# The first layer's seven products of pair 1 issued ahead of the last products with values

## The chip, the cores and the metric

The kernel runs on one core of a Trainium2 chip. The metric is the device time of one execution in microseconds (us), lower being better. The core has four computing engines that work side by side, each strictly through its own list of instructions: TensorE (PE in the profile; PEld is its loading of weights), VectorE (DVE), ScalarE (ACT) and GpSimd (POOL). SyncE (SP) issues most transfers (DMAs), also in a fixed order. An instruction that waits holds up everything behind it in its own list.

## The reference

All numbers are float32. A batch of 32 sequences of 112 rows (x, width 256) attends to its own context of 375 rows, with 16 heads of 64; then a mixture of 8 experts, two for each row, is added. Cut to what matters:

```
def xattn(ctx, latents):                  # latents: x after a normalisation
    q = lat @ Wq
    k, v = split(concat([ctx_normed, lat]) @ Wkv)
    attn = softmax(q k^T * scale)
    return (attn @ v) @ Wout

x = x + tanh(g_xattn) * xattn(ctx, layernorm(x))

xf = layernorm(x)                         # 3584 rows
top2 of softmax(xf @ gate_w), renormalised
h = gelu(xf @ w1[e] + b1[e])              # 256 -> 1024
y = h @ w2[e] + b2[e]                     # 1024 -> 256
x = x + tanh(g_ffn) * (sum of the two experts' y, weighted)
```

## The kernel before

The kernel has two stages that overlap at their seam.

**Attention** is a loop over 128 units `n` (32 sequences of 4 units). A unit computes scores, a softmax in the tile `ex`, and a transposition of it that goes through memory: `send_blocks(n)` writes `ex` to the memory tile `turned` in four DMAs (L526), `take_blocks(n)` reads it back as `exT[n]` (L533). `attend(j)` then makes the products with values for two units, 2j and 2j+1, into the PSUM tile `ps_o` (L546), and ScalarE copies the result to `outT` (L563). `project(i)` multiplies a slab of 128 rows of `outT` by Wout (L583), and `residual(i)` adds it to x on VectorE (L593), takes the row statistics (L241, L242), sends the slab to `out` on SyncE (L596), and leaves a root for GpSimd (L603, L605). When a slab is done its rows are routed: gate scores, the two best experts, places in the lists of the experts (among them the small matmuls L693 and L694, which need counts from GpSimd, L686), and a scatter of the rows to the memory tile `xg`.

**Experts** work on blocks of rows from `xg`, in pairs of blocks, 256 rows. Pair 0 is computed plainly (`hidden_plain`, L1047; `second_plain`, L1062), inside and just behind the last units of attention. Pairs 1 to 20 use a scheme with seven half-sized products in place of eight, in both layers:

- `fetch_rows(t)` reads a pair's rows into `xs` (L934); `turn_rows(t)` transposes them on TensorE (L1022) and copies them to `xsT` (L1026), on VectorE for pairs 1 and 2 and on ScalarE after that;
- `rows_sums(t)` makes the four sums `xt` on GpSimd (L1038);
- `fetch_first(t)` issues the seven weight tiles of the first layer (`w`, `w_s`, L987), behind a read of the biases (L948), all on SyncE; a tile has one buffer, so the fetch for pair t+1 waits for the products of pair t;
- `hidden_pair(t)` makes seven products (L1111, four matmuls each, all in PSUM tiles of one tag with four buffers), one copy on ScalarE (L1121), seven adds on VectorE (L1122 to L1130) and eight Gelus on ScalarE (L1118);
- `hidden_sums`, `second_pair`, `out_pair` and `fetch_second` do the same for the second layer; for pair 0 `combine(0)` ends the work (L1095, L1096, and the scatter L1072).

After the pairs come single blocks. The order of the work on every engine is written out by hand: the program order of the calls is the order on each engine. Between the attention loop and the loop over pairs stands the stretch that is changed. `pieces_of(6)` in that loop runs six more small parts of the routing of the last two slabs. `now()` empties the list of postponed GpSimd operations. The pair loop begins, for t = 1, with

```
hidden_pair(t)
fetch_first(t + 1)
turn_rows(t + 1, nc.scalar.copy if t > 1 else None)
if t + 1 < PAIRS:
    rows_sums(t + 1)
pieces_of(6)
```

In the last two turns of the attention loop the transfers on SyncE are, in order: block 126 of `exT`, the first-layer weights of pair 1, the four writes of block 127, its read into `exT`, and the second-layer weights of pair 1 with the rows of pairs 2 and 3.

Of the kernel before, what the change touches and what calls it, by code (L numbers as in the profile page):

```python
# [23 lines left out]
def kernel(  # L24
# [152 lines left out]
    if True:  # L177
# [360 lines left out]
        def attend(j):  # L538

            g, i = divmod(j, NG)  # L540
            ps = ps_m.tile([P, 2, 2 * S], F32, tag="m", name=f"ps_o_{j}")
            for r in range(2):
                for x in range(2):
                    for c, (_, m) in enumerate(keys):
                        for y in range(2):
                            nc.tensor.matmul(  # L546
                                ps[y * DH : (y + 1) * DH, r, x * S : (x + 1) * S].rearrange(
                                    "p (a i) -> p a i", a=QB
                                ),
                                lhsT=vv[j][:m, c, x, r, y * DH : (y + 1) * DH],  # L550
                                rhs=exT[2 * j + x][:m, :, r, c, y, :Q],
                                start=(c == 0),
                                stop=(c == NCK - 1),
                            )

            t, end = 2 * g * S, 2 * (g + 1) * S
            while t < end:
                slab, at = divmod(t, P)
                n = min(P - at, end - t)
                if slab not in outT:  # L560
                    outT[slab] = soft.tile([P, NP, P], F32, tag="outT", name=f"outT_{slab}", bufs=3)
                o = t - 2 * g * S
                nc.scalar.copy(outT[slab][:, i::NG, at : at + n], ps[:, :, o : o + n])  # L563
                t += n
# [9 lines left out]
        def project(i):  # L574

            g, j = group[i]
            if j == 0:
                xr[g] = rows.tile([P, groups[g], 2, C], F32, tag="xr", name=f"xr_{g}")
                nc.gpsimd.memset(xr[g][:, :, :, D + 2 :], 0.0)
            ps_p[i] = ps_m.tile([P, D], F32, tag="m", name=f"ps_p_{i}")  # L580
            heads = outT.pop(i)
            for c in range(NP):
                nc.tensor.matmul(  # L583
                    ps_p[i],
                    lhsT=heads[:, c, :],
                    rhs=wo_sb[:, c, :],
                    start=(c == 0),
                    stop=(c == NP - 1),
                )
# [376 lines left out]
        def fetch_first(t):  # L966

            e, new = found["e", t] = expert_of(t)
            fetch_biases(t, e, found["weights"], 2, (0,))
            if t < PAIRS:  # L970
                s1_, s2_, s3_, s4_ = (
                    (f"s{n + 1}", ws1[bass.ds(e, 1), place].rearrange("o p f -> p (o f)"))
                    for n, place in enumerate((3, 0, 1, 2))
                )
                a11, a12, a22 = (
                    (n, half_of_w1(e, k, h)) for n, k, h in (("11", 0, 0), ("12", 1, 0), ("22", 1, 1))
                )
                order_ = (a11, s2_, s3_, s1_, a22, a12, s4_)
            else:
                if t == PAIRS:  # L980
                    new_weights("21", [P, 512], "s3")
                order_ = [
                    (n, half_of_w1(e, k, h))
                    for n, k, h in (("11", 0, 0), ("12", 1, 0), ("21", 0, 1), ("22", 1, 1))
                ]
            for n, src in order_:
                nc.sync.dma_start(wt[n], src, **new)  # L987
# [29 lines left out]
        def turn_rows(t, copy=None):  # L1017
            n = 2 if t < PAIRS else 1
            ps = ps_m.tile([P, KD, n, P], F32, tag="m", name=f"ps_x_{t}")
            for k in range(KD):  # L1020
                for b in range(n):
                    nc.tensor.transpose(ps[:, k, b, :], xs[t][:, b, k * P : (k + 1) * P], ident)  # L1022
            xsT[t] = found["tiles" if t > 0 else "early"].tile(
                [P, KD, 2, P], F32, tag="xsT", name=f"xsT_{t}"
            )
            (copy or nc.vector.tensor_copy)(xsT[t][:, :, :n, :], ps)  # L1026

        def rows_sums(t):

            x = xsT[t]  # L1030
            v = xt[t] = found["tiles"].tile([P, 4, P], F32, tag="xt", name=f"xt_{t}")
            for o, l, r in (
                (v[:, 0], x[:, 0, 1], x[:, 0, 0]),
                (v[:, 1], x[:, 1, 1], v[:, 0]),
                (v[:, 2], x[:, 1, 1], x[:, 0, 1]),
                (v[:, 3], x[:, 1, 0], v[:, 1]),
            ):
                nc.gpsimd.tensor_tensor(o, l, r, ALU.subtract)  # L1038
# [19 lines left out]
        def second_plain(b):  # L1058
            banks.append(banks.pop(0))
            ps = psy[0, b] = banks[-1][:, 0, :D]  # L1060
            for f in range(NF):
                nc.tensor.matmul(  # L1062
                    ps,
                    lhsT=hid[0][:, f, b, :],
                    rhs=found["w2"][:, f, :],
                    start=(f == 0),
                    stop=(f == NF - 1),
                )
# [31 lines left out]
        def hidden_pair(t):  # L1100


            h = hid[t] = found["tiles"].tile([P, NF, 2, P], F32, tag="h", name=f"h_{t}")
            x, v = xsT[t], xt[t]
            H = NF // 2
            h11, h12, h21, h22 = (h[:, i : i + H, b, :] for i in (0, H) for b in range(2))

            def product(n, w, r):
                ps = ps_m.tile([P, H, P], F32, tag="m", name=f"ps_h_{t}_{n}")
                for c in range(H):  # L1110
                    nc.tensor.matmul(  # L1111
                        ps[:, c, :], lhsT=wt[w][:, c * P : (c + 1) * P], rhs=r, start=True, stop=True
                    )
                return ps

            def gelu(lo):
                for f in range(lo, lo + H):
                    nc.scalar.activation(h[:, f], h[:, f], AF.Gelu, bias=bias[t][0][:, f : f + 1])  # L1118

            add = nc.vector.tensor_tensor  # L1120
            nc.scalar.copy(h11, product(1, "11", x[:, 0, 0]))  # L1121
            add(h12, product(6, "s2", v[:, 1]), h11, ALU.add)  # L1122
            add(h21, product(7, "s3", v[:, 2]), h12, ALU.add)
            ps = product(5, "s1", v[:, 0])
            add(h22, ps, h21, ALU.add)
            add(h12, ps, h12, ALU.add)  # L1126
            add(h21, product(4, "22", v[:, 3]), h21, ALU.add)
            gelu(H)
            add(h11, product(2, "12", x[:, 1, 0]), h11, ALU.add)
            add(h12, product(3, "s4", x[:, 1, 1]), h12, ALU.add)  # L1130
            gelu(0)
# [224 lines left out]
        def do(parts):  # L1356
            for part in parts:
                part()
# [251 lines left out]
        def pieces_of(n):  # L1610
            for _ in range(min(n, len(todo))):
                do(todo.pop(0))

        now()
        for b in range(2):
            second_plain(b)
        attend(LAST // 2 - 1)
        for u in range(2):
            project(i + u)
        rows_sums(1)  # L1620
        for u in range(2):
            residual(i + u)
            now()
        for t in range(1, PAIRS):
            hidden_pair(t)
            fetch_first(t + 1)
            turn_rows(t + 1, nc.scalar.copy if t > 1 else None)
            if t + 1 < PAIRS:
                rows_sums(t + 1)
            pieces_of(6)  # L1630
            hidden_sums(t)
            if t > 1:
                second_pair(t - 1)
                out_pair(t - 1)
                fetch_second(t)
            else:
                combine(0)
                do(found.pop("sums"))
            if t + AHEAD == EARLY:
                pieces_of(len(todo))  # L1640
                do(outgoing)
                del outgoing[:]
            if t + AHEAD == EARLY + 1:
                for e in range(E):
                    r = number("behind", 0, e, PADS)
                    nc.sync.dma_start(xg[bass.ds(r, P), :], pad)
            fetch_rows(t + AHEAD)
            if outgoing:
                outgoing.pop(0)()
# [65 lines left out]
```

## Time and profile before

| what | value |
|---|---|
| time of three runs | 2052.3, 2056.42, 2056.62 us (median 2056.42) |
| the profiled execution | 2051.52 us, of which its span is 2049.8 us |
| mean granted clock of TensorE | 0.987 of full speed |
| TensorE busy | 1960.6 us, 96% of the span |
| VectorE, ScalarE, GpSimd busy | 66%, 56%, 48% |
| memory traffic | 211 GB/s on average over the span |
| TensorE waiting for the last transposed block in the products with values | 6.63 us, once |

Durations that follow are those of the one profiled execution. A timeline row gives the start in us from the span's start, the duration, engine, line of the kernel, operation, the tile written and the tiles read (numbers of buffers left out), the type and the count of instructions merged into the row; brackets hold the idle time of the engine before it and who ended that. A matmul in float32 is recorded as two instructions. A row by stretches gives how long each engine was busy within the stretch, then the clock granted to TensorE (1.00 is full speed), the share of the DMA engines in use and what they moved.

### The profile page before, as it was taken

What the parts mean: (1) busy time and instruction counts of PE and PEld (TensorE: products, weight loads), DVE (VectorE), ACT (ScalarE), POOL (GpSimd) and SP (SyncE); (2) the same over time, 40 slices, a digit from 0 to 9 for tenths busy, and PEclk for the clock granted to TensorE, in tenths of its full rate; (3) what the DMA queues carried; (4) which work ended last, traced back from release to release, by engine and by line L of the source; (5) the groups of instructions that cost most, each with busy time, mean ns of one, the idle gap of its engine ahead of it and who ended that gap; (6) DMA issues with size and microseconds to landing.
All of it is one profiled execution on the core that took longest, in us unless ns stands there. A gap on an engine that the chain in (4) does not pass through costs nothing. (4 is left out here: it accounts for less than half of the span.)

```text
span 2049.8 us, 41104 instructions
## 1 busy us (share of the span) xinstructions
PE 1960.6 (96%) x14352; PEld 1501.5 (73%) x14352; DVE 1348.0 (66%) x2417; ACT 1155.5 (56%) x2718; POOL 992.3 (48%) x1467
## 2 busy tenths in 40 slices
PE   8999999999999999999999999999988799799998
PEld 4676767676667676766777676667766799799887
DVE  6777776868776767677777777786764476455211
ACT  5666666566666656666666666666644234344333
POOL 5534333435355645655456646542332377757322
PEclk9999999999999999999999999999998899999999
DMA  7766665666687878788778878875666476599773
GB/s 215 204 214 198 181 201 170 190 180 202 192 247 216 270 214 249 231 254 234 231 224 250 242 227 232 260 201 165 200 191 201 127 222 176 148 326 294 203 222 53
DMA packets 261057, 433.40 MB, mean 211 GB/s; under 512 B 30729, under 2 KB 149073, under 8 KB 244465
## 3 DMA queue, kind: packets, MB, share of 16 engines
q1 hardware_dynamic: 248384, 414.37, 67.7%
q0 software_dynamic: 11328, 15.33, 3.9%
q8 instruction: 115, 1.88, 0.4%
q10 hardware_dynamic: 1136, 1.05, 0.2%
q14 instruction: 94, 0.76, 0.1%
HBM read 301.37 MB, written 172.28 MB: 231 GB/s over the span
## 5 line engine op out<-in xcount | busy, mean ns | idle before, releaser
L501 ACT ACTIVATE ex<-bank,nmx 128x512 f32<-128x512 f32 x512 | 348.3, 689 | 264.3 <-DVE nmx L492 264.3
L515 ACT ACTIVATE ex<-ex,rc 128x512 f32<-128x512 f32 x512 | 342.5, 720 | 202.9 <-DVE rc L512 201.3
L492 DVE TENSOR_REDUCE nmx<-bank 128x2 f32<-128x974 f32 x256 | 286.1, 1158 | 122.7 <-PE bank L482 122.7
L520 DVE STREAM_TRANSPOSE ex<-ex 128x1024 f32<-128x1024 f32 x256 | 315.0, 1230 | 28.4 <-ACT ex L515 28.4
L422 POOL TENSOR_TENSOR kT<-tmpk,kT 128x487 f32<-128x487 f32 x63 | 76.9, 1220 | 376.9 <-ACT kT L440 376.9
L412 PEld LDWEIGHTS ps_v<-wkv_s,tT 128*128 128x128 f32 x1536 | 190.1, 192 | 79.4 <-DVE kT L446 37.4
L482 PE MATMUL bank<-kT,qTs 64*128 64x487 f32 x1024 | 243.7, 594 | 0.0
L546 PE MATMUL ps_o<-exT,vv 128*64 128x112 f32 (+1 forms) x4096 | 213.7, 262 | 7.9 <-DMA exT<-turned 6.6
L412 PE MATMUL ps_v<-wkv_s,tT 128*128 128x128 f32 x1536 | 199.9, 278 | 13.2 <-DVE kT L446 11.7
L546 PEld LDWEIGHTS ps_o<-exT,vv 128*64 128x64 f32 (+1 forms) x4096 | 199.5, 137 | 16.3 <-DMA exT<-turned 6.8
L446 DVE TENSOR_TENSOR vv<-ps_v,vv 128x512 f32<-128x512 f32 x192 | 131.8, 687 | 108.1 <-PE ps_v L412 87.1
L406 PE MATMUL ps_k<-tT,wkv_s 128*128 128x487 f32 x378 | 181.0, 583 | 13.8 <-DVE vv L446 13.1
L412 PEld LDWEIGHTS ps_v<-wkv,kvT 128*128 128x128 f32 x1024 | 129.7, 192 | 72.9 <-issue 66.2
L422 POOL TENSOR_TENSOR vv<-tmpv,vv 128x512 f32<-128x512 f32 x64 | 81.4, 1271 | 188.3 <-ACT vv L440 188.0
L1072 POOL DMA_INDIRECT out_dram<-y,xs x60 | 93.4, 1557 | 162.0 <-DVE y L1096 92.2
L482 PEld LDWEIGHTS bank<-kT,qTs 64*128 64x128 f32 x1024 | 88.1, 186 | 103.3 <-issue 92.4
L446 DVE TENSOR_TENSOR kT<-ps_k,kT 128x487 f32<-128x487 f32 x189 | 123.3, 657 | 31.3 <-PE ps_k L406 26.1
L1300 POOL TENSOR_TENSOR piece<-piece 128x128 f32<-128x128 f32 x256 | 116.9, 457 | 55.1 <-DMA piece<-in_L_ffn_w_dram 39.3
L412 PE MATMUL ps_v<-wkv,kvT 128*128 128x128 f32 x1024 | 141.8, 282 | 0.0
L406 PE MATMUL ps_k<-kvT,wkv 128*128 128x487 f32 x252 | 130.2, 598 | 0.0
L333 PE MATMUL ps_q<-kvT,wq_sb 128*128 128x224 f32 x512 | 120.0, 356 | 1.4 <-ACT kvT L321 0.7
L1118 ACT ACTIVATE h<-h,b 128x256 f32<-128x256 f32 x160 | 66.2, 495 | 97.1 <-DVE h L1126 67.6
(296 smaller groups left out, 3689.2 us busy)
## 6 DMA issues: line engine op xcount, KB each, us to landing
turned<-ex SPq DMA_DIRECT2D x512, 256.0 KB
exT<-turned SPq DMA_DIRECT2D x128, 1024.0 KB
w<-in_L_ffn_w_dram SPq DMA_DIRECT2D x132, 256.0 KB
w_s<-ws SPq DMA_DIRECT2D x80, 256.0 KB
w_t<-ws SPq DMA_DIRECT2D x80, 256.0 KB
w_b2x<-in_L_ffn_w_dram SPq DMA_DIRECT2D x38, 512.0 KB
ws<-piece SPq DMA_DIRECT2D x64, 256.0 KB
cin<-in_ctx_dram SPq DMA_DIRECT2D x32, 336.0 KB
```

Source lines behind the costliest of these rows:

```text
L333: nc.tensor.matmul(ps, lhsT=wq_sb[:, k, i * P : (i + 1) * P], rhs=kvT[g][:, k, :, SC:NK], start=(k == 0), stop=(k == KD - 1),)
L406: nc.tensor.matmul(ps, lhsT=w[:, 0, i * P : (i + 1) * P], rhs=x[:, :NK], start=True, stop=True)
L412: nc.tensor.matmul(ps[:, c, :], lhsT=x[:, c * P : (c + 1) * P], rhs=w[:, 1, i * P : (i + 1) * P], start=True, stop=True,)
L422: nc.gpsimd.tensor_tensor(v[o], v[l], v[r], ALU.add)
L446: nc.vector.tensor_tensor(v[at], product(n, w, x), v[at], ALU.add)
L482: nc.tensor.matmul(ps[:, j, :NK], lhsT=qT[b // 2, i][r, b % 2].rearrange("p a i -> p (a i)"), rhs=kT[b, i][r, :], start=True, stop=True,)
L492: nc.vector.tensor_reduce(nmx[b, i], pss[b, i][:, :, :NK], AX.X, ALU.max, negate=True)
L501: nc.scalar.activation(exs[n % 2][:, :, p, :, j, :], ps[:, j, :].rearrange("p (c k r) -> p k c r", c=NCK, r=QW), AF.Exp, bias=nmx[b, i][:, ...
L515: nc.scalar.mul(t, t, rc[:, j : j + 1])
L520: nc.vector.transpose(t, t)
L546: nc.tensor.matmul(ps[y * DH : (y + 1) * DH, r, x * S : (x + 1) * S].rearrange("p (a i) -> p a i", a=QB), lhsT=vv[j][:m, c, x, r, y * DH : ...
L1300: nc.gpsimd.tensor_tensor(o, l, r, op) for o, l, r, op in ops
```

## The change

In the stretch between the two loops, the sums of the rows of pair 1 and its seven products of the first layer are issued ahead of the last call of `attend`, where they stood behind the two last projections (the sums) and at the head of the pair loop (the products). The loop over pairs skips the call for t = 1. With the products go the copy and the Gelus on ScalarE and the adds on VectorE that belong to `hidden_pair(1)`. It issues no DMA. Nothing is added or left out.

```
         for b in range(2):
             second_plain(b)
+        rows_sums(1)
+        hidden_pair(1)
         attend(LAST // 2 - 1)
         for u in range(2):
             project(i + u)
-        rows_sums(1)
         for u in range(2):
             residual(i + u)
             now()
         for t in range(1, PAIRS):
-            hidden_pair(t)
+            if t > 1:
+                hidden_pair(t)
             fetch_first(t + 1)
             turn_rows(t + 1, nc.scalar.copy if t > 1 else None)
             if t + 1 < PAIRS:
```

More of the change, by code (lines that the diff above doesn't have):

```diff
@@ L1616 @@
             second_plain(b)
+        rows_sums(1)
+        hidden_pair(1)
         attend(LAST // 2 - 1)
@@ L1619 @@
             project(i + u)
-        rows_sums(1)
         for u in range(2):
@@ L1624 @@
         for t in range(1, PAIRS):
-            hidden_pair(t)
+            if t > 1:
+                hidden_pair(t)
             fetch_first(t + 1)
```

## The prediction

> **What bounds the kernel now.** I read the 40 slices first (TensorE is busy 8 or 9 tenths in almost all of them, so time is won only where it stands still or runs slowly), then TensorE in order of time around the changed lines, then the busy time in stretches of 1 us for the clock and the transfers, then the other engines' timelines. The last entry of the chain of waits is only the closing scatter (1.25 us), and it says nothing about this place. TensorE's timeline here has start, duration, line, tiles, count, and in brackets the idle time before it with its releaser:
>
> ```profile
> 1576.53 7.07 PE L1062 MATMUL bank<-w,h 128*128 128x256 f32 x32
> 1583.53 0.99 PE L546 MATMUL ps_o<-exT,vv 128*64 128x112 f32 x16
> 1591.15 4.75 PE L546 MATMUL ps_o<-exT,vv 128*64 128x112 f32 x48 [6.63 <-DMA exT<-turned]
> 1595.83 7.67 PE L583 MATMUL ps_p<-wo_sb,outT 128*128 128x256 f32 x32
> 1603.34 1.05 PE L1111 MATMUL ps_h<-xsT,w 128*128 128x128 f32 x8
> ...
> 1609.59 0.60 PE L1022 MATMUL ps_x<-ident,xs 128*128 128x128 f32 x4
> 1610.03 0.29 PE L693 MATMUL ps_pos<-both,before 128*128 128x16 f32 x2
> 1613.44 0.39 PE L694 MATMUL ps_pos<-had,ones 128*128 128x16 f32 x2 [3.12 <-POOL had L686]
> 1613.69 1.83 PE L1111 MATMUL ps_h<-xsT,w 128*128 128x128 f32 x8
> ```
>
> The reader is to see a hole of 6.63 us: after the first 16 records of the last products with values, TensorE waits for the last transposed block (exT). The seven products of pair 1 (L1111, from 1603.34 to the transposes at 1609.59, that is **6.25 us**) stand behind that wait and do not need it. A matmul of this type is two records, so the 56 records are the 28 matmuls of seven products. The stretches (span, PE, PEld, DVE, ACT, POOL, granted clock, DMA share, GB/s) show two more things:
>
> ```profile
> 1582.00:1583.00 1.00, 1.00 (x6) 0.88 (x5) 0.00 (x0) 0.00 (x0) 0.00 (x0) 1.00 1.06 383
> 1585.00:1586.00 1.00, 0.00 (x0) 0.00 (x0) 0.00 (x0) 0.00 (x0) 0.00 (x0) 1.00 0.24 90
> 1586.00:1587.00 1.00, 0.00 (x0) 0.00 (x0) 0.00 (x0) 0.00 (x0) 0.00 (x0) 0.82 0.00 0
> 1592.00:1593.00 1.00, 1.00 (x14) 1.00 (x13) 0.00 (x0) 0.00 (x0) 0.00 (x0) 0.50 1.10 354
> 1596.00:1597.00 1.00, 1.00 (x3) 0.82 (x4) 0.00 (x0) 0.54 (x2) 0.00 (x0) 0.56 1.02 340
> 1615.00:1616.00 1.00, 1.00 (x7) 1.00 (x7) 0.51 (x3) 0.39 (x1) 0.34 (x2) 0.50 0.00 0
> ```
>
> The hole halves TensorE's clock until 1596.6, and the DMA engines move nothing at all between 1586 and 1587.
>
> **Part 1: can the seven products start at 1583.5?** They need three things. The sums of the rows (xt) ran on GpSimd from 1577.50 to 1579.3; there the move only swaps them with a memset of 0.10 us, free. Their weights are issued on the Sync queue from 1572.93 to 1579.37, ahead of the last turned blocks. From 1572 the stretches sum to 3086 KB by 1582; queued ahead of the weights were about 1270 KB (rows, a block of exT, a slab of x, less what had moved), and the seven tiles are 1835 KB, so in order of issue the last lands at about 1582. Even out of order nothing was outstanding at 1586, and the seventh product needs its tile only at 1583.5 + 6 x 0.89 = 1588.9. PSUM: the four buffers rotate, and VectorE, idle there, frees one per 0.69 us against 0.89 us per product. So they run from 1583.5 to 1589.8 at full clock.
>
> **Part 2: the products with values and the projection.** The first 16 records take 0.99 us, to 1590.8. The last block still lands at 1591.15, since no DMA has moved. A wait of 0.4 us is left, too short for the clock to fall. The other 48 records then cost 48/64 of the 3.30 us that 64 records took at 1569.31 with a full clock, 2.5 instead of 4.75 us: end at 1593.65, **2.2 us** earlier. ScalarE now has pair 1's copy and its eight Gelus ahead of the two outT copies. In the trace the Gelus end 9.0 us after the first product (1612.33 against 1603.34), so at 1592.5, before the copies are due. The projection loses its slow start: 7.07 us, as for the 32 records of the same form at 1576.53, instead of 7.67. It ends at 1600.7; the second residual on VectorE starts at S = 1600.95 instead of 1603.54, **2.6 us** earlier.
>
> **Part 3: what is late next.** Before, turn_rows(2) stood behind the seven products, its copy to xsT behind seven adds on VectorE (ending at 1611.08), GpSimd's row sums behind the copy, and the routing matmul L694 behind those (1613.44). Now the transposes follow the projection directly (to 1601.3). VectorE does the residual's three operations (1.16 us after S) and then the copy, to 1602.8. GpSimd does vex and rsx of the residual (1602.2 to 1603.1), then row sums and counts: from row sums to L694 the trace has 1613.44 - 1611.16 = 2.28 us. L694 comes at 1605.5, **7.9 us** earlier than 1613.44. This is the 6.25 us of products, plus 2.6 us from the clock and the projection, less about 0.9 us because GpSimd's root and VectorE's statistics are now in the chain.
>
> The queue that does not move by 7.9 us is Sync. fetch_first(2) stands behind the residual's write to out, so it moves by 2.6 us only: its first tile is issued at 1603.6 instead of 1606.22. Before, the seven tiles moved from 1607.1 to about 1613.4, so now from 1604.5 to 1610.8, the first complete at about 1605.6, with perhaps half a us until its semaphore. The first product of pair 2 can wait for that, 0.5 to 1 us. But its seventh product ran at 1620.79, which becomes 1612.9, 2 us after its tile. And the end of pair 2's products is set by VectorE: its adds begin at 1619.06 behind place, normed and combine(0), which hang on L694. So this wait is hidden up to about 2 us; beyond that each us is lost.
>
> After that I found nothing fixed in time: TensorE is full from 1630 to 1780 but for holes that other engines of the same loop set, and the 12.74 us stall at 1793 (eight dependent pad transfers on Sync, from 1770.39) starts behind the weight fetches of its own iteration, so it moves along. The sum: **-7.9 us**.
>
> **The clock, by rule and by row.** The Trainium skill (TensorE: Matmul & The Clock Gate, "The HAM clock gate") says that one idle window of about 3.4 us halves the clock and about as much sustained work restores it. It speaks against the change at one point: TensorE is now idle from 1601.3 to 1605.5, 4.2 us, so by the page's figures pair 2 would begin cold and lose up to half of 3.4 us; an estimate from that page is then -6.2. The trace shows that the shorter idle time before (3.12 us) had already been enough: clock 0.50 at 1615, eight records in 1.83 instead of 1.05 us. So the loss is in the old sum too, and VectorE's adds hide it. I take the row: no new loss.
>
> **Bounds of what the trace does not show.** The meeting of pair 2's weights with its products costs between 0 and 2.5 us (at worst every product waits for its tile). VectorE and GpSimd block each other by chance around 1623 (one normalisation of 128x256 takes 3.99 us there against 0.41 at 1616.17): if the two meet differently, up to 3.6 us less or some 1.3 us more (one more GpSimd operation of 1.27 us). I take none for both, since all parties hang on L694.
>
> **Rivals.**
> *Pair 2's weights bind* (chance 0.12). If what matters is the fetch behind the residual, only the 2.6 us of Part 2 remain, or between 2.6 and 5: 2051.5 to 2054 on the scale of the median. For it: Sync's order and a margin under 1 us at the first tile. Against it: the tiles were there 7 us before the last product of pair 2, which waits for VectorE.
> *The gain is given back later* (0.04): a wait on Sync or a transfer that is due anyway, no change, 2056. Against it: no row after 1613 shows a wait for an event that this change leaves where it is.
> *Pair 1's weights are late* (0.06, the slower side). TensorE works in order, so if the seventh product waits until time t, the last products with values, the outT copies behind the Gelus, the projection, the routing and the fetch of pair 2 all slip. The new residual starts at t + 0.9 + 3.5 + 7.3 = t + 11.7. With Part 3's 5.3 us saved after it, it breaks even at t = 1597, and at t = 1603 the kernel is 6 us slower, 2062. It decides if the fetch takes over 17 us after its last issue (1579.37). Against it: the zero of the DMA stretch at 1586. That the move has no effect is out: the order of every engine here is written by hand, and the diff changes TensorE's.
> *More than forecast* (0.07): the 3.99 us operation no longer collides, about -11.5 us, 2045.
>
> **How the numbers follow.** The forecast has 0.71. Its sum is made against the profiled execution, 2051.52 us (span 2049.8 and 1.7 around it): 2043.6. That run lies at the fast end of the three timed (2052.3 to 2056.62, median 2056.42); on the median's scale it is 2048.5, which I predict. The range reaches from the best case seen at the scale's fast end (2043) to the weights' case (2052.5). A change of 0.2% is 4.1 us, about what a measurement of this kernel can tell from none. Faster takes the forecast, the larger gain and about a third of the weights' case: 0.82. Same takes the rest of that and the gain given back: 0.12. Slower: 0.06.
>
> **What would show it.** After: L1111 x8 directly behind the L1062 records, no hole over 1 us before L546, clock 1.00 through L546 and L583, L546's last 48 records in about 2.5 us; the first residual's statistics 2 to 3 us earlier, L694 at about 1605.5, and pair 2's seven products ending near 1614. A wait of TensorE for w or w_s at pair 1 would prove the slower rival; one of over 2 us at pair 2 the weights' case; an equal shift of 7 to 8 us at L694 that is gone by 1793 would make the prediction wrong in Part 3's last sentence.

## The result, and the profile after

The changed kernel takes 2044.89 us (median of 16 runs, 2042.0 to 2051.75), the kernel before 2053.63 us (16 runs, 2052.05 to 2057.05). The ratio is 0.9959 with a 95% interval of 0.9951 to 0.9967, that is 8.4 us less, between 6.8 and 10.1. The profiled execution (2044.3 us) has a span of 2042.5 us. Four of the 16 runs lie at 2049.2 to 2051.8 us, 4 to 7 us above the median; there is no trace of them, so what they lost stays open.

TensorE's timeline of the changed kernel, in the columns of before (start, duration, line, tiles, records, idle time before it with its releaser):

```profile
1574.63 7.07 PE L1062 MATMUL bank<-w,h 128*128 128x256 f32 x32
1581.54 1.05 PE L1111 MATMUL ps_h<-xsT,w 128*128 128x128 f32 x8
...
1587.88 3.30 PE L546 MATMUL ps_o<-exT,vv 128*64 128x112 f32 x64
1591.11 7.17 PE L583 MATMUL ps_p<-wo_sb,outT 128*128 128x256 f32 x32
1598.12 0.60 PE L1022 MATMUL ps_x<-ident,xs 128*128 128x128 f32 x4
...
1602.70 0.61 PE L694 MATMUL ps_pos<-had,ones 128*128 128x16 f32 x2 [3.84 <-POOL had L686]
1603.67 2.05 PE L1111 MATMUL ps_h<-xsT,w 128*128 128x128 f32 x8 [0.37 <-DMA w<-in_L_ffn_w_dram]
1605.51 4.75 PE L1111 MATMUL ps_h<-xt,w_s 128*128 128x128 f32 x24
```

The seven products follow pair 0's second layer without a gap. The products with values run in one piece: 64 records in 3.30 us, where 16 and 48 of them had stood on the two sides of the hole. The projection needs 7.17 instead of 7.67 us. The stall in pair 13 is still there, 12.17 us long where it was 12.74; it now ends at 1782.12 instead of 1793.37.

The stretches of 1 us show the clock (third number from the right). Where the clock switches within a stretch, the mean gives the moment: 0.80 puts the fall at 1602.6, 0.79 the return at 1609.4.

```profile
1592.00:1593.00 1.00, 1.00 (x7) 0.87 (x6) 0.00 (x0) 0.00 (x0) 0.00 (x0) 1.00 1.04 331
1602.00:1603.00 1.00, 0.30 (x2) 0.30 (x2) 0.00 (x0) 0.00 (x0) 0.84 (x5) 0.80 0.80 264
1605.00:1606.00 1.00, 1.00 (x6) 1.00 (x5) 0.74 (x3) 0.19 (x1) 0.10 (x1) 0.50 0.70 266
1609.00:1610.00 1.00, 1.00 (x9) 1.00 (x9) 0.69 (x1) 0.00 (x0) 0.68 (x1) 0.79 0.33 96
```

It is full through the values and the projection, and half in the first part of pair 2's products, now until 1609.4.

Two profiles of even the same code differ by a few us in where this stretch of the program begins. So I count from the start of pair 0's second layer (the first L1062 record, 1576.53 before and 1574.63 after). All rows below are from the profiles' timelines. "Pair 1" and "pair 20" are the starts of the second layers of the first and the last pair with seven products (the first records of L1168), "rest" is from there to the end of the span.

| us from the first L1062 record | 2nd residual (L593) | L694 | pair 1 | pair 20 | rest |
|---|---|---|---|---|---|
| before | 27.01 | 36.91 | 53.30 | 326.36 | 146.9 |
| change | 23.70 | 28.07 | 44.61 | 316.97 | 150.9 |
| difference | -3.3 | -8.8 | -8.7 | -9.4 | +4.0 |

The gain is there in full at L694, and stays up to the last pair. What the +4.0 of the last column is worth is a matter of the experiments.

### The profile page after: what moved, and what is told of

Same layout as the page of the kernel before. It is cut to its first block, busy times and chain, and to the rows that moved or that the text cites. A ratio compares the mean times of both kernels' runs of the same rounds, so it can differ in the third digit from the quotient of the medians.

```text
span 2042.5 us, 41105 instructions
## 1 busy us (share of the span) xinstructions
PE 1959.8 (96%) x14352; PEld 1501.2 (73%) x14352; DVE 1347.7 (66%) x2417; ACT 1156.2 (57%) x2718; POOL 992.0 (49%) x1467
## 5 line engine op out<-in xcount | busy, mean ns | idle before, releaser
L406 PE MATMUL ps_k<-tT,wkv_s 128*128 128x487 f32 x378 | 181.1, 583 | 13.9 <-DVE vv L446 13.8
```

What stands on the lines that cost most here:

```text
L406: nc.tensor.matmul(ps, lhsT=w[:, 0, i * P : (i + 1) * P], rhs=x[:, :NK], start=True, stop=True)
```

## The experiments

**e1: the sums alone.** Against the kernel before; the products stay at their old place.

```
             second_plain(b)
+        rows_sums(1)
         attend(LAST // 2 - 1)
...
-        rows_sums(1)
```

> Only the sums of pair 1's rows stand ahead of the last products with values; the seven products stay where they were before. Both theories: no change from before (within 1 us), since on GpSimd the sums change places with one memset of 0.10 us; the hole of 6.6 us stays. It also shows how much the stretch of single blocks at the end (157 us before, 161 us after) differs between profiles of the same code.

Measured: ratio 0.9998 (0.9988 to 1.0007). The sums are worth nothing. This profile is also a second one of the old order: second residual 27.12, L694 37.02, pair 20 at 326.16, within 0.2 us of before (pair 1, at 52.50, is 0.8 us earlier; the operation of 3.99 us is the subject of a paragraph below). Its rest is 150.8 us, so the 146.9 of before was a quick one, and the +4.0 in the table above is not an effect that a single pair of profiles can show. Over all the profiles of this study, with the same code there, the rest was 146.9 to 153.0 us. In it TensorE waits now and then for a weight transfer, 0.2 to 1.6 us each.

**e2: the seven products behind the values, ahead of the projections.** Against the change.

```
         rows_sums(1)
-        hidden_pair(1)
         attend(LAST // 2 - 1)
+        hidden_pair(1)
```

> The seven products stand behind the last products with values and ahead of the two projections. Theory (they fill the wait for the last block): the hole of 6.6 us and the half clock stay, the second residual starts 6.25 us later than before, L694 at about its old place plus 0.8 us; time 0 to 1.5 us over before. Rival (what matters is only that nothing stands between the projections and the transposes of pair 2): about 5 us under before.

Measured: 0.9995 (0.9987 to 1.0004), that is -1.0 us with an interval from -2.7 to +0.8. TensorE's timeline of this kernel:

```profile
1585.30 0.99 PE L546 MATMUL ps_o<-exT,vv 128*64 128x112 f32 x16
1592.29 4.03 PE L546 MATMUL ps_o<-exT,vv 128*64 128x112 f32 x48 [6.01 <-DMA exT<-turned]
1596.25 1.16 PE L1111 MATMUL ps_h<-xsT,w 128*128 128x128 f32 x8
```

The hole is back, and what the products save behind the residual they cost ahead of it: the second residual comes at 31.43 (+4.4), L694 at 35.80 (-1.1). The rival's 5 us are excluded. My own numbers were somewhat too high: the residual slipped by 4.4 and not 6.25 us, since the wait for the block was 0.6 us shorter, the clock came back sooner in the values (4.03 us instead of 4.75), and the projections ran at the full clock. In this profile the last pair comes 3.0 us earlier than before (323.39 instead of 326.36), which is more than the time shows; why stays open.

**e3: the hole filled with work that nobody needs.** Against the kernel before, in its order, with seven matmuls whose results are not used.

```
             second_plain(b)
+        for f in range(7):
+            idle(4 + f)
         attend(LAST // 2 - 1)
```

> Order of before, with seven matmuls of ones by ones (128x512, about 0.87 us each, results not used) ahead of the last products with values. Theory (the clock is one term, 2.6 us, of the gain): no half clock in the products with values, their last 48 records in 2.5 instead of 4.75 us, everything behind 2 to 3 us earlier, time 2 to 3 us under before. Rival (the clock's part is hidden by other engines): 0. Rival (the clock is the whole gain): over 6 us under before.

Measured: 0.9983 (0.9976 to 0.9989), -3.5 us (-4.9 to -2.3). In its timeline the fillers (L1367) take 6.17 us and the values follow in one piece:

```profile
1581.85 6.17 PE L1367 MATMUL ps_idle<-ones 128*128 128x512 f32 x14
1587.95 3.30 PE L546 MATMUL ps_o<-exT,vv 128*64 128x112 f32 x64
1591.18 7.17 PE L583 MATMUL ps_p<-wo_sb,outT 128*128 128x256 f32 x32
```

The second residual is at 23.46 and L694 at 33.35, both 3.6 us earlier than before, and pair 20 at 322.28 is 4.1 earlier. Of the 3.6 us, 2.8 are the clock: the 48 records behind the block take 2.5 (48/64 of 3.30) instead of 4.75 us and the projection 7.17 instead of 7.67. The other 0.8 is the block: it was there 13.8 us after the first L1062 record at the latest, against 14.6 before. It comes at a slightly different moment in every profile (14.7 in e1, 14.0 in e2, 15.4 in e8). Useless work makes the kernel faster, since it keeps the clock up. The clock is thus one term of the gain, 2.8 us by these rows, and not the whole.

**e4 and e12: one step further ahead.** Against the change; the sums and the products stand before pair 0's second layer; the same kernel twice, the second time beside the change.

```
+        rows_sums(1)
+        hidden_pair(1)
         for b in range(2):
             second_plain(b)
-        rows_sums(1)
-        hidden_pair(1)
```

> The seven products and their sums one step further ahead, before pair 0's second layer. Theory (pair 1's weights land within about 6 us of the start of pair 0's second layer, at about the pace of the products): small waits only, for the sums and single weight tiles, together 1 to 2 us; the products with values begin that much later; time 0.5 to 1.5 us over the change. Rival (weights land late, only just in time for the change): waits of 5 us or more for w or w_s, time over 4 us above the change.

> As e4, on the chip of the change. The profile of e4 had a wait of 2.2 us for one weight tile and its timed runs were some 4 us over the change of another chip. Theory (weights land with the products, small waits): 1 to 3 us over the change on the same chip. Rival (in many executions they land later): 4 us or more over it.

Measured: 0.9982 (0.9974 to 0.9989) and 0.9978 (0.9969 to 0.9988), so 3.7 and 4.5 us under before, and 3.95 us over the change in the medians of one chip (2049.61 against 2045.66). In TensorE's timeline of e4:

```profile
1574.57 0.60 PE L1022 MATMUL ps_x<-ident,xs 128*128 128x128 f32 x4
1577.41 1.13 PE L1111 MATMUL ps_h<-xsT,w 128*128 128x128 f32 x8 [2.24 <-DMA w<-in_L_ffn_w_dram]
```

The first product waits 2.24 us for its tile (1.52 in e12), the six others hardly at all. So pair 1's weights do land at the pace of the products, and the first was there 4.5 us before the change asks for it: 2.84 us after these transposes began (1577.41 - 1574.57), where the change begins its products 7.35 us after them (1581.54 - 1574.19), with pair 0's second layer in between. Late weights would thus cost what they are late, and in the profiles of the change (here and e9) they are not. My 0.5 to 1.5 us over the change were too low: in the profiles the last pair is 2.8 to 3.5 us later than in the change, counted from the transposes. The medians' 3.95 us do not contradict this, as the two intervals reach 2 and 3 us to either side; whether there is more than the wait stays open.

**e5, e6, e7: what is late next.** All against the change. e5 issues pair 2's weights ahead of the residuals' writes. e6 puts five routing parts of the last group but one (counts, places, gates, slots, scatter list) into the time when VectorE and GpSimd are idle. e7 does both.

```
         hidden_pair(1)
+        pieces_of(5)                       # e6, e7
         attend(LAST // 2 - 1)
         for u in range(2):
             project(i + u)
+        fetch_first(2)                     # e5, e7
         for u in range(2):
             residual(i + u)
...
             if t > 1:
                 hidden_pair(t)
-            fetch_first(t + 1)
+                fetch_first(t + 1)         # e5, e7
...
-            pieces_of(6)
+            pieces_of(6 if t > 1 else 1)   # e6, e7
```

> The change, and pair 2's first-layer weights issued on SyncE ahead of the two residuals' writes. Theory (this fetch is hidden in the change; the begin of pair 1's second layer hangs on GpSimd behind L694): the wait of 0.37 us and the slow start of pair 2's products lessen, their end comes up to 1 us earlier, pair 1's second layer begins at the same distance; time 0 to 1 us under the change. Rival (pair 2's weights bind): 1.5 us or more under the change.

> The change, and the five routing parts of the last but one group (counts, places, gates, slots, scatter list) ahead of the last products with values, where VectorE and GpSimd stand idle. Theory (L694, behind the row sums on GpSimd, is what is late next): TensorE no longer waits 3.8 us for it; pair 0's end on VectorE and the scatter start some 5 us earlier, pair 2's products still wait for their weights; time 2 to 4 us under the change. Rival (something else, such as the weights or the residual's root, is as late): within 1 us of the change.

> Both of the last two. Theory (two waits end at almost the same time, so that taking one away brings little and both more): pair 2's products begin 3 us or more earlier than in the change, time 4 to 7 us under the change, more than the sum of the two alone. Rival (the two are independent): the sum of the two alone. Rival (neither binds): within 1 us of the change.

Measured against before: e5 0.9964 (0.9951 to 0.9978), e6 0.9960 (0.9945 to 0.9975), e7 0.9951 (0.9935 to 0.9967); the change has 0.9959. None of the three is to be told from the change by these intervals; e7 stands apart from e5 and e6 by its median (2041.47 against 2045.09 and 2044.51). The profiles show why, if one counts from the second residual to the first gate matmul behind pair 2's products (L630), which leaves out when the last block came: 17.98 us in the change (17.80 in e9), 17.09 in e5, 17.21 in e6, 12.13 in e7. One wait removed brings 0.9 or 0.8 us, both 5.8. From there to pair 1's second layer the profiles differ by the clock: 1.87 us in e6, whose first gate matmuls took 0.61 us at the full clock, and 2.93 or 2.94 in the change, e5 and e7, where they took 1.02 at half. In e6, TensorE no longer waits for L694, and the weights take its place:

```profile
1597.88 0.60 PE L1022 MATMUL ps_x<-ident,xs 128*128 128x128 f32 x4
1603.72 2.05 PE L1111 MATMUL ps_h<-xsT,w 128*128 128x128 f32 x8 [5.24 <-DMA w<-in_L_ffn_w_dram]
```

On VectorE the 5 us of e6's theory did come (pair 0's first L1095 stands at 26.0 instead of 31.1 us from the first L1062 record), but not in the time. For e7 the theory held in mechanism, with less time than the 4 to 7 us expected: its median lies 11.0 us under that of before beside it, the change's 8.7.

**e8: the second hole filled.** Three matmuls of no use between pair 2's transposes and L694.

```
             turn_rows(t + 1, nc.scalar.copy if t > 1 else None)
+            if t == 1:
+                for f in range(3):
+                    idle(4 + f)
```

> The change, with three matmuls of ones by ones (results not used) between the transposes of pair 2 and L694, so that TensorE's idle time of 3.8 us is filled to 1.2 us. Theory (the half clock in pair 2's products is hidden behind VectorE and GpSimd): their 56 records end 1 to 1.5 us earlier, pair 1's second layer begins where it did; time within 0.5 us of the change. Rival (the half clock costs what it takes): 1 to 1.7 us under the change.

Measured: 0.9961 (0.9948 to 0.9974), the same as the change. The idle time fell to 1.27 us, and there was another of 0.86 us for the weights. The clock fell all the same:

```profile
1606.84 2.04 PE L1111 MATMUL ps_h<-xsT,w 128*128 128x128 f32 x8 [0.86 <-DMA w<-in_L_ffn_w_dram]
```

```profile
1606.00:1607.00 1.00, 0.16 (x1) 0.19 (x2) 0.17 (x1) 0.00 (x0) 0.81 (x5) 0.84 1.00 293
1610.00:1611.00 1.00, 1.00 (x10) 1.00 (x10) 0.96 (x3) 0.00 (x0) 0.56 (x2) 0.96 0.92 317
```

It stayed low for 3.4 us (1606.7 to 1610.1) instead of 6.8 (1602.6 to 1609.4): from the first of pair 2's products to the next transposes it took 7.87 us instead of 9.11. The timed runs, with an interval of 2.7 us to either side, can't tell these 1.2 us from nothing. The profile can: from the second residual to the first gate matmul it is 17.59 us, against 17.98 in the change and 17.80 in e9, so 0.2 to 0.4 us of the 1.2 got through. That speaks for the theory. The test is not a clean one, as the clock was not kept.

**e9, e10, e11: on one chip.** e9 is the change, e10 is e7 once more, e11 is e10 with `turn_rows(2, nc.scalar.copy)` and `rows_sums(2)` ahead of the residuals.

> The change itself, on the chip of the three runs beside it. Expected: 8 to 9 us under before, and in its profile the last block of exT landing within 1 us of the end of the seven products. It is the measure for the next three.

> Pair 2's fetch and the five routing parts both ahead, as in e7. Theory (two waits that end together): 3 to 5 us under the change on the same chip. Rival (the two are independent, each worth under 1 us): within 1 us of the change.

> As e10, with the transposes and row sums of pair 2 ahead of the residuals and their copy on ScalarE. Theory (the 1.4 us that TensorE still waits for VectorE's copy behind the residual is on the path): pair 2's products begin 1 to 1.5 us earlier than in e10, time 0 to 1.5 us under e10. Rival (what follows hangs on the root of the residual and GpSimd): no change from e10.

Measured: e9 2045.66 us, 0.9958 (0.9945 to 0.9972); e10 2042.15 us, 0.9942 (0.9929 to 0.9956); e11 2044.55 us, 0.9959 (0.9945 to 0.9973). In e9's profile the block is again there when the seven products end. So e10 is 3.5 us under the change by the medians, about what e7 was under e5 and e6 (3.6 and 3.0); the intervals of e10 and e9 still overlap. It is the fastest version of the study, 9.0 to 14.6 us under before. In its profile pair 1's second layer comes 14.00 us after the second residual, against 20.74 in e9 (12.13 and 17.80 up to the first gate matmul).

e11 missed: its median is 2.4 us over that of e10, though the intervals overlap. VectorE's timelines, first of e10 and then of e11, show the operation behind the residual's statistics:

```profile
1599.90 0.66 DVE L1026 COPY xsT<-ps_x 128x512 f32<-128x512 f32 x1
1600.47 0.40 DVE L611 TENSOR_SCALAR xr<-x,mvx,rsx 128x256 f32<-128x256 f32 x1
```

```profile
1599.64 0.18 DVE L242 BATCH_NORM_AGGREGATE mvx<-stx 128x2 f32<-128x6 f32 x1
1602.59 0.41 DVE L611 TENSOR_SCALAR xr<-x,mvx,rsx 128x256 f32<-128x256 f32 x1 [2.77 <-POOL rsx L605]
```

Pair 2's products began 0.7 us earlier (25.12 against 25.84 from the first L1062 record). But on GpSimd the row sums now stand ahead of the residuals' roots, VectorE waits 2.77 us for a root, and the adds behind it are late: pair 1's second layer comes at 41.03 instead of 38.05. A move that helps one engine's list pushed something back on another's.

## Why the prediction was right

**Its sum.** Forecast -7.9 us, measured -8.4 (-10.1 to -6.8). The predicted time, 2048.5, is 3.6 us too high; 2.8 of that is its scale, as the median of the three runs known then was 2056.42 and that of 16 is 2053.63.

**Part 1, the start at once: right.** No wait, 6.34 us of products, and e4 puts the landing of the first tile 4.5 us before it was needed.

**Part 2, -2.6 us up to the second residual: right, -3.3 in the first profile.** The values took the predicted time at full clock. The durations in the prediction give 2.8 rather than 2.6: it leaves 0.25 us between the end of the projection and the residual, where the trace has 0.05. The projection took 0.1 us longer than forecast, and 0.5 us is the block, which was luck: in the change's profile it was there in time, while in the profiles of e5, e7 and e8 the wait is 0.97, 0.42 and 1.14 us. The residual stood at 23.70 to 25.06 in the eight profiles with the products in the new place (the change, e5 to e11); I had 24.4. That the clock was the cause of the 2.8 is shown by e3.

**Part 3, -5.3 us behind the residual: right.** From the second residual to L694 the trace has 9.90 us before and 4.37 after, so 5.53. The order on VectorE and GpSimd was as worked out, down to the statistics and the root that entered the chain. On GpSimd the row sums, which had waited for VectorE's copy, now follow the root at once (first row before, the others after):

```profile
1611.16 0.46 POOL L1038 TENSOR_TENSOR xt<-xsT 128x128 f32<-128x128 f32 x1 [5.50 <-DVE xsT L1026]
...
1599.88 0.57 POOL L605 TENSOR_TENSOR rsx<-vex,nhalf 128x1 f32<-128x1 f32 x1
1600.43 0.44 POOL L1038 TENSOR_TENSOR xt<-xsT 128x128 f32<-128x128 f32 x1
```

VectorE's timeline after:

```profile
1598.33 0.48 DVE L593 SCALAR_TENSOR_TENSOR x<-ps_p,tg,x 128x256 f32<-128x256 f32 x1 [2.29 <-PE ps_p L583]
1598.84 0.43 DVE L241 BATCH_NORM_STATS2 stx<-x 128x6 f32<-128x256 f32 x1
1599.31 0.18 DVE L242 BATCH_NORM_AGGREGATE mvx<-stx 128x2 f32<-128x6 f32 x1
1599.41 0.66 DVE L1026 COPY xsT<-ps_x 128x512 f32<-128x512 f32 x1
```

**The weights of pair 2: mechanism right, size nearly.** The wait at the first product is 0.37 us (0.72 in e9), forecast 0.5 to 1. That it is all but hidden is what e5 shows: with the wait gone the time is not to be told from the change's, and of the 0.9 us that its profile gains up to the first gate matmul, 0.5 lies ahead of the first add, where the two multiplications of `combine(0)` (L1096) took 1.26 us together instead of 1.82. e6 shows how near it stood: with L694 out of the way it becomes 5.24 us at once.

**The clock in pair 2's products: a term of the sum that was mis-sized, by little.** I took no new loss, since the clock had fallen there before too. It did fall again, but stayed low for 6.8 us instead of 3.4 (1613.9 to 1617.4 before), and the seven products took 9.11 us up to the next transposes instead of 8.38. VectorE, which I had as the only limit, then waited for TensorE twice between the first add and the fifth (first two rows before, the others after):

```profile
1619.06 0.68 DVE L1122 TENSOR_TENSOR h<-ps_h,h 128x512 f32<-128x512 f32 x1
1621.84 0.68 DVE L1127 TENSOR_TENSOR h<-ps_h,h 128x512 f32<-128x512 f32 x1
...
1608.31 0.68 DVE L1122 TENSOR_TENSOR h<-ps_h,h 128x512 f32<-128x512 f32 x1
1609.24 0.69 DVE L1123 TENSOR_TENSOR h<-ps_h,h 128x512 f32<-128x512 f32 x1 [0.25 <-PE ps_h L1111]
1610.30 0.69 DVE L1125 TENSOR_TENSOR h<-ps_h,h 128x512 f32<-128x512 f32 x1 [0.37 <-PE ps_h L1111]
...
1611.51 0.68 DVE L1127 TENSOR_TENSOR h<-ps_h,h 128x512 f32<-128x512 f32 x1
```

What follows hangs on the fifth add, which frees the first Gelus (L1127): ScalarE's eight Gelus, its copies for the gate, the gate's matmuls, the second layer. From the first add to the fifth it was 2.78 us before and 2.79 in e1, e2, e3 and e8, but 3.20 in the change and 3.02 in e9 (and 3.66 in e12, where the first product waits 0.93 us). So 0.2 to 0.4 us of the half clock got through in the change, not the 1.7 of the estimate by the Trainium skill (TensorE: Matmul & The Clock Gate, "The HAM clock gate").

**The operation of 3.99 us.** The rival that gave 3.6 us for a missed collision is out. It took 3.32 us in the change, and 0.41 in e1 and e5; from the first gate matmul (L630) to pair 1's second layer it was 3.18 us before, 2.27 in e1, 2.94 in e5 and 2.93 in the change. That leaves 0.9 us for it at the most, as the Gelus on ScalarE run beside it. The change and e5 are alike in spite of it, since the first gate matmuls ran at half the clock in both (1.02 us instead of the 0.61 of before and e1).

**The other rivals.** Late weights for pair 1 are excluded by e4 and by the change's own two profiles, for the executions that were profiled. A gain given back later is not seen up to pair 20 (-9.4 us). Whether some of it goes in the single blocks stays open: the three profiles with the products in the old place (before, e1, e3) have a rest of 146.9, 150.8 and 151.0 us, the change's two 150.9 and 151.0.

## What to carry to other kernels

Fill a wait for a late transfer with work that stands behind it and needs nothing from it, and then work out, queue by queue, what that work had been hiding. A hole costs more than its length, since the clock falls with it: here 6.6 us of waiting cost 2.8 us more. Where two waits end within a us of each other, try both cures together before either is given up: alone they brought 0.9 and 0.8 us up to the first gate matmul, together 5.8.

## What the runs showed that I had not expected

Matmuls whose results nobody uses made the kernel 3.5 us faster (2.3 to 4.9), and by the profile most of that is the clock. TensorE's clock fell in e8 although its longest idle time was 1.27 us, with another of 0.86 us soon after it. And behind the second hole it stayed at half for 3.4 us (before, e8) or for 6.8 us (the change), one or two windows of the Trainium skill's 3.4 us (TensorE: Matmul & The Clock Gate, "The HAM clock gate"), so that the time at half clock behind a hole differs from run to run by a factor of two.

The profiles show what goes with the one and with the other. Before, the clock fell at 1586.64, came back at 1596.88 and fell again at 1613.94:

```profile
1613.00:1614.00 1.00, 0.56 (x4) 0.56 (x5) 0.12 (x1) 0.00 (x0) 0.81 (x4) 0.97 1.00 361
```

That is 10.24 and 17.06 us apart, or 3 and 5 steps of 3.41 us. In all fourteen profiles the lengths and distances of the low stretches from 1540 to 1660 us come out as whole steps in the same way. Where the steps lie against the work differs from one execution to the next. Where TensorE's unbroken work behind the second hole began before the clock fell or at most 0.2 us after (before, e1, e3, e4, e8), it was low for one step; where that work began 0.7 to 3.2 us after (the change, e2, e5, e6, e9, e12), for two. So the 3.4 us of e8 may be the place of its steps as much as its shorter idle time.
